# Where register loads stand, the order of VectorE's work in odd halves, and how many groups of rows come singly, in a graph-network kernel

## The chip, the core and the metric

The kernel runs on one core of a Trainium2 chip. The metric is the device time of one execution in microseconds. Before the change it is 3714.35 us, the median of 11 executions (3708.14 to 4204.9 us).

## What is computed

One layer of message passing on a graph of 12500 nodes with 128 features and 400000 edges sorted by destination, in float32. For node features x and edge features ea (32 wide):

```
h   = relu(layernorm(x))
m_e = relu(concat(h[src_e], h[dst_e], ea_e) @ w1 + b1) @ w2 + b2
agg = segment_sum(m, dst)
out = x + GRU(agg, h)          # gates from agg @ w_ih + b_ih and h @ w_hh + b_hh
```

The first product splits by rows of w1 into A[src] + B[dst] + ea @ w1e, with A = h @ w1a and B = h @ w1b.

## The kernel before, in words

**Set-up.** A first stage normalizes all nodes, keeps h transposed in SBUF (`hT_all`, 128 x 12500) and writes the table A (one row of 512 bytes for each node) to device memory.

**Tiling.** The 400000 edges are 3125 tiles of 128. Eight tiles make a double group k (391 of them): two groups a = 0, 1 of four tiles, whose destinations lie in two windows of 32 nodes that stand 8 nodes apart. A unit u is half a double group: u = 2k + h, four tiles, 512 edges. The main loop runs over the 782 units and issues, for each, pieces of several later units, so that the engines work in a pipeline. "Program unit u" below means what the loop issues in its round u. Instructions of an engine run in the order in which they were issued.

**One double group, step by step, with the rounds in which it is issued:**
- `fetch(q)` (lines 479 to 489) loads, on SP's queue and for two double groups at once, the edge features `L` (rows 64 to 127 of a 128-row tile, L485) and the destinations `Ld`, broadcast to 32 partitions in each of two DMAs (L488). Three buffers each. It is issued in round 4q - 8.
- `onehot_T(k)` (L495): VectorE compares Ld with node numbers; the result is the upper half of L. Round 2k - 6.
- `window(k)`: VectorE copies 64 columns of h (`hw`, L514) at a place from a register; TensorE multiplies them with w1b (L517). `window_rows(k)` (L526): VectorE adds b1 in two instructions, into `RW`, whose lower half holds w1e. Both are issued in even rounds, in phases 1 and 3 of the round.
- `onehot(k)` (L544): VectorE makes the one-hot matrix for the sum over destinations. Odd rounds, ahead of the add.
- `pre(u)` (L592): TensorE forms B[dst] + b1 + ea @ w1e of a unit in PSUM, from L and RW. Round u - 3.
- `add(u)` (L617): VectorE adds A's rows `G`. `relu(u)` (L623): ScalarE writes the activation. Round u - 2.
- `seg(u)` (L636): TensorE sums over destinations. `take(k)` (L644, L645) copies the sums out.
- Each 14 double groups, `node(b)` finishes 512 nodes (lines 648 to 727) in some 15 small steps, one in each round.

**How A's rows arrive.** There are four ways:
- POOL gathers them: eight indirect DMAs of 128 rows for a double group (L146), into a ring of 7 buffers.
- SP fetches them one row at a time: 1024 DMAs of 512 bytes (L795), each at an address from a register, into the only buffer `G_sp`.
- ScalarE (L788) or VectorE (L790) copies columns of h out of `hT_all`, one edge at a time, 128 x 4 bytes each, at a place from a register, 1024 for a double group. TensorE then multiplies these columns with w1a and adds them in PSUM (L603), and `add` is not needed.
- The first ten double groups gather rows of x and normalize them.

43 double groups come singly: 19 by ScalarE, 18 by VectorE, 6 by SP, spread by `SPREAD` from double group 30 on (lines 85 to 93). The registers are loaded 32 at a time (L782) from a table of indices in SBUF; the next 32 are loaded where the last of the 32 before have been used. A job (one double group's 1024 singles) starts in round 30 at the earliest and is spread evenly, in steps of 2 or 4 singles, over the four phases of its rounds (`run_jobs`). A job of SP for double group k ends by round 2k - 8, and the next may start in round 2k + 2, when the activation has read `G_sp`. SP's jobs cover the rounds 30 to 112, 122 to 232, 242 to 352, 362 to 472, 482 to 592 and 602 to 714.

**What sets the order.** No scheduler moves anything: the rounds, the four phases in a round and the calls in `stages` are the order. A round is: phase 0 of the jobs; `take`; `stages`; phase 1 (and `window`); phase 2; `seg`; phase 3 (and `window_rows`, and a step of `node`).

Of the kernel before, what the change touches and what calls it, by code (L numbers as in the profile page):

```python
# [8 lines left out]
F32 = mybir.dt.float32  # L9
# [33 lines left out]
PLACE = 20  # L43
CH = PLACE * PAIR
LOAD = 32
STEP = {"act": 4, "dve": 4, "sp": 2}
SPREAD = {"act": 19, "dve": 18, "sp": 6}
NR = 12672

H_AT = 16512  # L50
# [6 lines left out]
def tile_gnn(ctx: ExitStack, tc: tile.TileContext, x, src, srcT, dstT, dstP, eaT, eaP, w1, b1, w2T, b2,  # L57
# [26 lines left out]

    mode, order = {}, {m: [] for m in SPREAD}
    for m, n in SPREAD.items():
        lo = JOBS0 + 15
        for i in range(n):
            k = lo + int((i + 0.5) * (NP - 2 - lo) / n)
            while k in mode:  # L90
                k += 1
            mode[k] = m
            order[m].append(k)
# [385 lines left out]
    def fetch(q):  # L479
        if q * QP >= NP:  # L480
            return
        n = min(QP, NP - q * QP)
        Ls[q] = p3.tile([128, QP * 512], F32, name="L")
        c = slice(q * QP * 512, (q * QP + n) * 512)
        nc.sync.dma_start(Ls[q][2 * V:, :n * 512], eaP[:, c])  # L485
        Ds[q] = p3.tile([2 * V, QP * 512], I32, name="Ld")
        for a in range(2):
            nc.sync.dma_start(Ds[q][V * a:V * (a + 1), :n * 512],  # L488
                              dstP[a:a + 1, c].to_broadcast([V, n * 512]))
# [6 lines left out]
                                None, op0=ALU.is_equal)  # L496


    bases, PB_ = {}, {}

    def window(k):
        if k >= NP:
            return
        b = k // BP
        if k % BP == 0:
            n = min(BP, NP - k)
            _, vals = nc.values_load_multi_w_load_instructions(
                base_i[0:1, b, 0:n], engines=[ET.DVE], min_val=0, max_val=LAST,
                skip_runtime_bounds_check_because="clamped above")
            for i, v in enumerate(vals):  # L510
                bases[k + i] = v
        hw = p3.tile([128, 2, V], F32, name="hw", bufs=2)
        s = hT_all[:, bass.ds(bases.pop(k), V + SHIFT)]
        nc.vector.tensor_copy(hw, bass.AP(tensor=s.tensor, offset=s.offset,  # L514
                                          ap=[list(s.ap[0]), [SHIFT, 2], [1, V]]))
        PB_[k] = ps2.tile([128, 512], F32, name="oh")
        nc.tensor.matmul(PB_[k][:2 * V, :D], hw.rearrange("p a v -> p (a v)"), w1b,  # L517
                         start=True, stop=True)

    def window_rows(k):  # L520
        if k >= NP:
            return
        pm = PB_.pop(k)
        for a in range(2):
            s = slice(V * a, V * (a + 1))
            nc.vector.tensor_tensor(RW[k % 4][s, a, :], pm[s, :D], b1b[s, :], op=ALU.add)  # L526

    def onehot(k):
        if k >= NP:
            return  # L530
        t0, t1 = tiles(k)
        OH[k] = OHB[k % len(OHB)]
        for a in range(2) if k == 0 else (None,):
            if a is None:
                o, s = OH[k].rearrange("p j a v -> p a j v"), slice(t0, t1)
                d = dloc[:, s].rearrange("p (a j) -> p a j", a=2)[:, :, :, None]
                shape = [128, 2, GRP, V]
                i = iota[:, None, None, :]
            else:
                e = min(t1, (a + 1) * GRP)  # L540
                o, d = OH[k][:, :e - a * GRP, a, :], dloc[:, a * GRP:e, None]
                shape = [128, e - a * GRP, V]
                i = iota[:, None, :]
            nc.vector.tensor_tensor(o, d.to_broadcast(shape), i.to_broadcast(shape),  # L544
                                    op=ALU.is_equal)
# [222 lines left out]
        nc.sync.dma_start(at[r:r + 1, :], src[t0 * 128:(t0 + PAIR) * 128].rearrange(  # L768
            "(o e) -> o e", o=1))

    def one_by_one(m, k):
        et = {"act": ET.Activation, "dve": ET.DVE, "sp": ET.SP}[m]
        r = by_hand.index(k)
        if m == "sp":
            G[k] = pj[0].tile([128, GRP, 2, D], F32, name="G_sp", bufs=1)
            rows = G[k].bitcast(U8)
        else:
            hand[k] = pj[0].tile([128, PAIR * 128], F32, name=f"HE_{m}")
            he = hand[k].bitcast(U8)
        for e0 in range(0, PAIR * 128, LOAD):  # L780
            low, high = (0, ROW * (N - 1)) if m == "sp" else (H_AT, H_AT + 4 * (N - 1))
            _, vals = nc.values_load_multi_w_load_instructions(  # L782
                at[r:r + 1, e0:e0 + LOAD], engines=[et], min_val=low, max_val=high,
                skip_runtime_bounds_check_because="src holds numbers of nodes")
            for i, v in enumerate(vals):
                e = e0 + i
                if m == "act":
                    nc.scalar.copy(he[:, e * 4:e * 4 + 4], h_bytes[:, bass.ds(v - H_AT, 4)])  # L788
                elif m == "dve":
                    nc.vector.tensor_reduce(he[:, e * 4:e * 4 + 4],  # L790
                                            h_bytes[:, bass.ds(v - H_AT, 4), None],
                                            AX.X, ALU.max)
                else:
                    a, j = divmod(e // 128, GRP)
                    nc.sync.dma_start(rows[e % 128:e % 128 + 1, j, a, :],  # L795
                                      A_bytes[bass.ds(v, ROW)].rearrange("(o f) -> o f", o=1))
                if i % STEP[m] == STEP[m] - 1:
                    yield


    jobs = {}
    for m, kl in order.items():
        start = 2 * JOBS0
        for k in kl:
            end = 2 * k - (8 if m == "sp" else 4)
            jobs.setdefault(start, []).append((m, k, end - start))
            start = end if m != "sp" else 2 * k + 2
    live = {}

    PH = 4  # L810

    def run_jobs(u, phase):
        if u == 2 * JOBS0 and phase == 0:
            early.close()
            pj.append(late.enter_context(tc.tile_pool(name="pj", bufs=2, side="right")))
        if phase == 0:
            for m, k, span in jobs.get(u, ()):
                live[m] = [one_by_one(m, k), u, span, PAIR * 128 // STEP[m], 0]
        for m, job in list(live.items()):
            it, start, span, steps, done = job  # L820
            want = -(-steps * ((u - start) * PH + phase + 1) // (span * PH))
            while job[4] < want:
                job[4] += 1
                if next(it, "end") == "end":
                    del live[m]
                    break


    asked = [RAW]
# [9 lines left out]

    gathers(0)  # L840
    for q in range(2):
        fetch(q)
    for k in range(3):
        window(k)
        window_rows(k)


    def stages(u):
        if u + 7 >= 0:
            raw_stats(u + 7)  # L850
        if u + 6 >= 0:
            raw_fin(u + 6)
            raw_h(u + 6)
        if u % 2 == 0:
            onehot_T(u // 2 + 3)
        elif u > -7:
            onehot(u // 2 + 3)
        if u + 4 >= 0:
            raw_turn(u + 4)
        if u + 3 >= 0:  # L860
            pre(u + 3)
        if u + 2 >= 0:
            add(u + 2)
            relu(u + 2)

    for u in range(-7, 0):
        stages(u)
# [12 lines left out]
    for u in range(NU):  # L880
        k, h = divmod(u, 2)
        gathers(u)
        if h == 0:
            if k % QP == 0:
                fetch(k // QP + 2)
            if k % BP == 0 and k:
                nodes_left.append([node(k // BP - 1), 0])
            if k % PLACE == 1:
                indices(k // PLACE + 2)
            if k % PLACE == 5:  # L890
                place(k // PLACE + 1)
                dst_tile(k // PLACE + 2)
            if k == NP - 20:
                check_windows()
        for r in range(2 * u, min(2 * u + 2, NJ)):
            job_indices(r)
        if u == 2 * JOBS0 - 2:
            nc.vector.tensor_scalar(at, at, place_of[:, 0:1], place_of[:, 1:2],
                                    op0=ALU.mult, op1=ALU.add)

        def other(phase):
            run_jobs(u, phase)
            if h == 0 and phase == 1:
                window(k + 3)
            if h == 0 and phase == 3:
                window_rows(k + 3)
            if phase == 3:
                step(nodes_left)

        other(0)  # L910
        if h == 0:
            take(k - 1)
        stages(u)
        other(1)
        other(2)
        seg(u)
        if u == 0:
            node_setup()
        other(3)
# [173 lines left out]
```

## Time and profile before

| | |
|---|---|
| median of 11 | 3714.35 us |
| the profiled execution | 3722.88 us, of which its span is 3721.1 us |
| mean TensorE clock granted | 0.78 |
| POOL's gathers from A | 2704, 0.956 us each, 0.30 us apart |
| ScalarE's single copies | 19456, 189 ns each, overlapping; 1966.1 us busy in all |
| VectorE's single copies | 18432, 146 ns each, overlapping; 1338.4 us busy in all |
| VectorE's adds of A's rows | 676, 683 ns each |
| SP's single rows | 6144, from 224.5 to 3430.6 us |
| idle time of POOL that ended with ScalarE's activation | 181.8 us |

The span is one execution on the chip. "Busy" counts the time in which an engine had at least one operation running; overlapping ones count once. "Issue" as the end of an idle time means that nothing the profile shows ended it: the engine's sequencer was occupied. Register loads and the issuing of DMAs run on the sequencers and are not counted as busy. "SPq" is SP's sequencer.

### The profile page before, as it was taken

The page shows a single profiled execution, that of the slowest core. Times are in us where ns is not written, and L with a number is a line of the kernel's source. Part 1 is how long each engine was busy: PE and PEld are TensorE (multiplying, and loading weights), DVE is VectorE, ACT ScalarE, POOL GpSimd, SP SyncE. Part 2 cuts the span into 40 slices and gives each one's busy share as a digit, 9 for nine tenths or more (in the row PEclk, how much of TensorE's full clock was granted, in tenths as well). Part 3 has the DMA queues.
Part 4 walks back from the last instruction along what each step waited for, and adds up shares of the span by engine and source line. Part 5 has one row for each costly group of instructions (what it writes and reads, how often), then busy time and mean ns, then how long its engine had stood idle before and what let it go on. Part 6 is the DMA issues. An engine that isn't in the chain of part 4 may idle for free. (4 is left out here: it accounts for less than half of the span.)

```text
span 3721.1 us, 94893 instructions
## 1 busy us (share of the span) xinstructions
PE 2652.2 (71%) x13578; PEld 1641.5 (44%) x13578; DVE 2629.5 (71%) x22515; ACT 2515.5 (68%) x20936; POOL 2657.9 (71%) x2789
## 2 busy tenths in 40 slices
PE   6684665767776777677777767777776677677768
PEld 6452333444443444444444434444444444344435
DVE  7765556677777676767777777777777777777774
ACT  5455556667677777767777776777777777767772
POOL 7677646477777677777777777677777677777775
PEclk9897777777777877877787777777877877787779
DMA  6333222233333333333333333333333333333332
GB/s 201 83 92 81 74 66 75 71 90 84 90 85 89 81 87 86 87 86 87 94 86 87 87 90 84 81 88 88 93 88 89 81 89 86 89 84 90 86 87 65
DMA packets 157887, 325.92 MB, mean 88 GB/s; under 512 B 65058, under 2 KB 77133, under 8 KB 157256
## 3 DMA queue, kind: packets, MB, share of 16 engines
q0 software_dynamic: 88992, 182.43, 19.5%
q1 hardware_dynamic: 68119, 137.33, 13.8%
q14 instruction: 520, 4.25, 0.4%
q8 instruction: 112, 1.84, 0.2%
q10 hardware_dynamic: 144, 0.07, 0.0%
HBM read 305.74 MB, written 13.84 MB: 86 GB/s over the span
## 5 line engine op out<-in xcount | busy, mean ns | idle before, releaser
L146 POOL DMA_INDIRECT G<-A,src_i x2704 | 2583.9, 956 | 1005.7 <-issue 769.0
L788 ACT COPY HE_act<-hT_all 128x4 uint8 x19456 | 1966.1, 189 | 584.7 <-issue 582.0
L790 DVE TENSOR_REDUCE HE_dve<-hT_all 128x4 uint8 x18432 | 1338.4, 146 | 718.5 <-issue 708.3
L592 PE MATMUL pre<-RW,L 128*128 128x256 f32 x3128 | 1141.8, 494 | 131.1 <-DVE G L617 99.6
L592 PEld LDWEIGHTS pre<-RW,L 128*128 128x128 f32 x3128 | 681.8, 242 | 439.2 <-issue 295.4
L517 PE MATMUL oh<-w1b,hw 128*64 128x128 f32 x782 | 210.8, 360 | 893.1 <-DVE hw L514 889.0
L623 ACT ACTIVATE RB<-G 128x512 f32<-128x512 f32 x676 | 424.8, 628 | 335.3 <-DVE G L617 84.5
L636 PE MATMUL seg<-RB,OH 128*32 128x129 f32 x6250 | 646.5, 342 | 0.0
L517 PEld LDWEIGHTS oh<-w1b,hw 128*64 128x64 f32 x782 | 90.2, 163 | 1046.2 <-DVE hw L514 1023.8
L617 DVE TENSOR_TENSOR G<-pre,G 128x512 f32<-128x512 f32 x676 | 461.7, 683 | 10.1 <-PE pre L592 0.3
L636 PEld LDWEIGHTS seg<-RB,OH 128*32 128x32 f32 x6250 | 351.0, 131 | 236.7 <-issue 137.5
L495 DVE TENSOR_SCALAR L<-Ld,node_of 64x512 f32<-64x512 int32 x391 | 192.0, 491 | 86.2 <-DMA Ld<-in_dstP 70.9
L526 DVE TENSOR_TENSOR RW<-oh,b1b 32x128 f32<-32x128 f32 x782 | 217.4, 278 | 48.4 <-PE oh L517 39.9
L644 DVE COPY sums<-seg 64x128 f32<-64x128 f32 x391 | 107.6, 275 | 84.0 <-PE seg L636 78.8
L544 DVE TENSOR_TENSOR OH<-dloc,iota 128x256 f32<-128x256 f16 (+1 forms) x392 | 162.6, 415 | 0.5 <-issue 0.2
L667 PEld LDWEIGHTS nd<-spot,sums 64*128 64x128 f32 x782 | 152.7, 300 | 12.9 <-issue 12.9
L667 PE MATMUL nd<-spot,sums 64*128 64x40 f32 x782 | 156.8, 385 | 0.0
L645 ACT CAST dcol<-seg 64x1 f16<-64x1 f32 x391 | 59.3, 152 | 136.8 <-DVE sums L644 136.3
L631 PE MATMUL seg<-zrow 1*64 1x129 bf16 x391 | 106.4, 272 | 0.0
L146 POOL DMA_INDIRECT G<-in_x,src_i x77 | 73.0, 948 | 25.1 <-issue 22.9
L514 DVE COPY hw<-hT_all 128x64 f32 x391 | 82.5, 211 | 11.1 <-issue 8.3
L631 PEld LDWEIGHTS <-zrow 1*64 1x64 bf16 x391 | 43.4, 111 | 93.2 <-issue 93.2
(151 smaller groups left out, 1521.4 us busy)
## 6 DMA issues: line engine op xcount, KB each, us to landing
G_sp<-A SPq DMA_DIRECT2D x6144, 0.5 KB
L<-in_eaP SPq DMA_DIRECT2D x195, 256.0 KB
Ld<-in_dstP SPq DMA_DIRECT2D x390, 128.0 KB
G<-A,src_i POOLq DMA_INDIRECT x2704
xb<-in_x SPq DMA_DIRECT2D x28, 256.0 KB
out<-xb SPq DMA_DIRECT2D x28, 256.0 KB
xs<-in_x SPq DMA_DIRECT2D x11, 512.0 KB
A<-asb SPq DMA_DIRECT2D x11, 512.0 KB
```

What stands on the lines that cost most here:

```text
L146: nc.gpsimd.indirect_dma_start(out=G[k][:, j, a, :], out_offset=None, in_=table, in_offset=bass.IndirectOffsetOnAxis(ap=src_i[c][:, i:i + ...
L495: nc.vector.tensor_scalar(Ls[k // QP][:2 * V, c], Ds[k // QP][:, c], node_of[:, k:k + 1], None, op0=ALU.is_equal)
L517: nc.tensor.matmul(PB_[k][:2 * V, :D], hw.rearrange("p a v -> p (a v)"), w1b, start=True, stop=True)
L526: nc.vector.tensor_tensor(RW[k % 4][s, a, :], pm[s, :D], b1b[s, :], op=ALU.add)
L544: nc.vector.tensor_tensor(o, d.to_broadcast(shape), i.to_broadcast(shape), op=ALU.is_equal)
L592: nc.tensor.matmul(PP[u][:, 2 * i:2 * i + 2, :], Ls[k // QP][:, c0:c0 + 128], RW[k % 4], start=True, stop=not raw)
L617: nc.vector.tensor_tensor(RT[u], PP.pop(u), RT[u], op=ALU.add)
L623: nc.scalar.activation(o[:, :, :D], RT.pop(u), AF.Relu)
L636: nc.tensor.matmul(SEG[k][V * a:V * (a + 1), :D + 1], OH[k][:, j, a, :], RB[u % 3][:, (j % 2) * 2 + a, :D + 1], start=False, stop=all(b != ...
L667: nc.tensor.matmul(pt[:, bass.ds(offs[i], V + SHIFT)], sums[:, i, :], spot, start=False, stop=i == n - 1)
L788: nc.scalar.copy(he[:, e * 4:e * 4 + 4], h_bytes[:, bass.ds(v - H_AT, 4)])
L790: nc.vector.tensor_reduce(he[:, e * 4:e * 4 + 4], h_bytes[:, bass.ds(v - H_AT, 4), None], AX.X, ALU.max)
```

## The change

- 49 double groups come singly: 22 by VectorE, 20 by ScalarE, 7 by SP. Their places are spread anew. VectorE's jobs start in round 31, ScalarE's in 47, SP's in 30. SP's jobs now cover the rounds 30 to 134, 144 to 238, 248 to 340, 350 to 444, 454 to 548, 558 to 650 and 660 to 754.
- VectorE's and ScalarE's jobs load 32 registers once in a round: VectorE's load stands after the add (and, in odd rounds, after the bias adds and the one-hot) and the last 7 singles of the 32 before; ScalarE's after the activation and the last 8. The other singles are spread over the four phases. SP loads as before and issues its rows evenly.
- `window`'s copy moves into even rounds ahead of the add, its matmul (`window_b`) stays in phase 1, and the bias adds (`window_rows`) move into the odd round after the add. `onehot` moves after the add too.
- The loads of Ld (`fetch_d`) are split from those of L and issued one fetch, four rounds, earlier; within a round they stand ahead of L's.

```diff
-STEP = {"act": 4, "dve": 4, "sp": 2}
-SPREAD = {"act": 19, "dve": 18, "sp": 6}
+
+TAIL = {"dve": 7, "act": 8}
+SPREAD = {"dve": 22, "act": 20, "sp": 7}
...
-        lo = JOBS0 + 15
+        lo, hi = {"dve": (JOBS0 + 3, NP - 14), "act": (JOBS0 + 11, NP - 6),
+                  "sp": (JOBS0 + 5, NP - 10)}[m]
         for i in range(n):
-            k = lo + int((i + 0.5) * (NP - 2 - lo) / n)
+            k = lo + int((i + 1) * (hi - lo) / n)
...
+        c = slice(q * QP * 512, (q * QP + n) * 512)
         Ls[q] = p3.tile([128, QP * 512], F32, name="L")
+        nc.sync.dma_start(Ls[q][2 * V:, :n * 512], eaP[:, c])
+
+    def fetch_d(q):
...
-        nc.sync.dma_start(Ls[q][2 * V:, :n * 512], eaP[:, c])
         Ds[q] = p3.tile([2 * V, QP * 512], I32, name="Ld")
...
+        HW[k] = hw
+
+    def window_b(k):
+        if k >= NP:
+            return
         PB_[k] = ps2.tile([128, 512], F32, name="oh")
-        nc.tensor.matmul(PB_[k][:2 * V, :D], hw.rearrange("p a v -> p (a v)"), w1b,
+        nc.tensor.matmul(PB_[k][:2 * V, :D], HW.pop(k).rearrange("p a v -> p (a v)"), w1b,
                          start=True, stop=True)
...
+    def behind(m, u):
+        if m in live:
+            live[m].run()
+            if live[m].e == PAIR * 128:
+                del live[m]
+        begin(m, u + 1)
+        if m in live:
+            j = live[m]
+            if j.loaded < PAIR * 128:
+                j.load(LOAD)
...
+    PARTS = (1, 2, 3, 0)
 
     def run_jobs(u, phase):
...
+        for m in ("act", "dve"):
+            if m in live:
+                n = max(0, len(live[m].vals) - TAIL[m])
+                live[m].run(TAIL[m] + n - -(-n // (4 - PARTS.index(phase))))
         if phase == 0:
...
+            begin("sp", u)
+        if "sp" in live:
+            j = live["sp"]
+            want = -(-PAIR * 128 * ((u - j.start) * 4 + phase + 1) // (j.span * 4))
+            while j.e < want:
+                if not j.vals:
+                    j.load(LOAD)
+                j.run(max(0, len(j.vals) - (want - j.e)))
...
         if u % 2 == 0:
             onehot_T(u // 2 + 3)
-        elif u > -7:
-            onehot(u // 2 + 3)
+            if u >= 0:
+                window(u // 2 + 3)
...
         if u + 2 >= 0:
             add(u + 2)
+        if u % 2 and u > -7:
+            if u > 0:
+                window_rows(u // 2 + 3)
+            onehot(u // 2 + 3)
+        if u + 2 >= 0:
+            behind("dve", u)
             relu(u + 2)
+            behind("act", u)
...
             if k % QP == 0:
+                fetch_d(k // QP + 3)
                 fetch(k // QP + 2)
...
         def other(phase):
             run_jobs(u, phase)
             if h == 0 and phase == 1:
-                window(k + 3)
-            if h == 0 and phase == 3:
-                window_rows(k + 3)
+                window_b(k + 3)
```

More of the change, by code (lines that the diff above doesn't have):

```diff
@@ L482, in fetch @@
         n = min(QP, NP - q * QP)
+        c = slice(q * QP * 512, (q * QP + n) * 512)
         Ls[q] = p3.tile([128, QP * 512], F32, name="L")
+        nc.sync.dma_start(Ls[q][2 * V:, :n * 512], eaP[:, c])
+    def fetch_d(q):
+        if q * QP >= NP:
+            return
+        n = min(QP, NP - q * QP)
         c = slice(q * QP * 512, (q * QP + n) * 512)
-        nc.sync.dma_start(Ls[q][2 * V:, :n * 512], eaP[:, c])
         Ds[q] = p3.tile([2 * V, QP * 512], I32, name="Ld")
@@ L496, in onehot_T @@
                                 None, op0=ALU.is_equal)
-    bases, PB_ = {}, {}
+    bases, PB_, HW = {}, {}, {}
     def window(k):
@@ L515, in window @@
                                           ap=[list(s.ap[0]), [SHIFT, 2], [1, V]]))
+        HW[k] = hw
+    def window_b(k):
+        if k >= NP:
+            return
         PB_[k] = ps2.tile([128, 512], F32, name="oh")
-        nc.tensor.matmul(PB_[k][:2 * V, :D], hw.rearrange("p a v -> p (a v)"), w1b,
+        nc.tensor.matmul(PB_[k][:2 * V, :D], HW.pop(k).rearrange("p a v -> p (a v)"), w1b,
                          start=True, stop=True)
@@ L769, in job_indices, with __init__, load, run @@
             "(o e) -> o e", o=1))
[L771 to L780, printed above, removed]
+    class Job:
+        def __init__(self, m, k, start, span):
+            self.m, self.k, self.start, self.span = m, k, start, span
+            self.e, self.loaded, self.vals = 0, 0, []
+            self.r = by_hand.index(k)
+            if m == "sp":
+                G[k] = pj[0].tile([128, GRP, 2, D], F32, name="G_sp", bufs=1)
+                self.to = G[k].bitcast(U8)
+            else:
+                hand[k] = pj[0].tile([128, PAIR * 128], F32, name=f"HE_{m}")
+                self.to = hand[k].bitcast(U8)
+        def load(self, n):
+            m = self.m
             low, high = (0, ROW * (N - 1)) if m == "sp" else (H_AT, H_AT + 4 * (N - 1))
+            et = {"act": ET.Activation, "dve": ET.DVE, "sp": ET.SP}[m]
             _, vals = nc.values_load_multi_w_load_instructions(
-                at[r:r + 1, e0:e0 + LOAD], engines=[et], min_val=low, max_val=high,
+                at[self.r:self.r + 1, self.loaded:self.loaded + n], engines=[et],
+                min_val=low, max_val=high,
                 skip_runtime_bounds_check_because="src holds numbers of nodes")
-            for i, v in enumerate(vals):
-                e = e0 + i
+            self.vals = list(vals)
+            self.loaded += n
+        def run(self, left=0):
+            while len(self.vals) > left:
+                v, e, m, to = self.vals.pop(0), self.e, self.m, self.to
+                self.e += 1
                 if m == "act":
-                    nc.scalar.copy(he[:, e * 4:e * 4 + 4], h_bytes[:, bass.ds(v - H_AT, 4)])
+                    nc.scalar.copy(to[:, e * 4:e * 4 + 4], h_bytes[:, bass.ds(v - H_AT, 4)])
                 elif m == "dve":
-                    nc.vector.tensor_reduce(he[:, e * 4:e * 4 + 4],
+                    nc.vector.tensor_reduce(to[:, e * 4:e * 4 + 4],
                                             h_bytes[:, bass.ds(v - H_AT, 4), None],
@@ L794, in one_by_one, with begin @@
                     a, j = divmod(e // 128, GRP)
-                    nc.sync.dma_start(rows[e % 128:e % 128 + 1, j, a, :],
+                    nc.sync.dma_start(to[e % 128:e % 128 + 1, j, a, :],
                                       A_bytes[bass.ds(v, ROW)].rearrange("(o f) -> o f", o=1))
-                if i % STEP[m] == STEP[m] - 1:
-                    yield
-    jobs = {}
+    starts = {}
     for m, kl in order.items():
-        start = 2 * JOBS0
+        start = 2 * JOBS0 + (m != "sp") + (16 if m == "act" else 0)
         for k in kl:
             end = 2 * k - (8 if m == "sp" else 4)
-            jobs.setdefault(start, []).append((m, k, end - start))
+            starts[m, start] = (k, end - start)
             start = end if m != "sp" else 2 * k + 2
     live = {}
-    PH = 4
+    def begin(m, u):
+        if (m, u) in starts:
+            live[m] = Job(m, starts[m, u][0], u, starts[m, u][1])
+    def behind(m, u):
[8 more added lines that the diff above has]
+                j.load(LOAD)
+            assert j.span * LOAD >= PAIR * 128
+    PARTS = (1, 2, 3, 0)
     def run_jobs(u, phase):
@@ L815, in run_jobs @@
             pj.append(late.enter_context(tc.tile_pool(name="pj", bufs=2, side="right")))
+        for m in ("act", "dve"):
+            if m in live:
+                n = max(0, len(live[m].vals) - TAIL[m])
+                live[m].run(TAIL[m] + n - -(-n // (4 - PARTS.index(phase))))
         if phase == 0:
[L817 to L826, printed above, removed]
+            begin("sp", u)
[6 more added lines that the diff above has]
+                j.run(max(0, len(j.vals) - (want - j.e)))
+            if j.e == PAIR * 128:
+                del live["sp"]
     asked = [RAW]
@@ L841, in tile_gnn @@
     for q in range(2):
+        fetch_d(q)
         fetch(q)
+    fetch_d(2)
     for k in range(3):
         window(k)
+        window_b(k)
         window_rows(k)
```

## The prediction

> **What bounds the kernel now.** I read the page's first table, the waits by engine in two windows, the timeline of SP's queue, and last the sizes of the register loads.
>
> The busy table alone names no bound: four engines stand at 68 to 71%.
>
> ```profile
> PE 2652.2 (71%) x13578; PEld 1641.5 (44%) x13578; DVE 2629.5 (71%) x22515; ACT 2515.5 (68%) x20936; POOL 2657.9 (71%) x2789
> ...
> L788 ACT COPY HE_act<-hT_all 128x4 uint8 x19456 | 1966.1, 189 | 584.7 <-issue 582.0
> L790 DVE TENSOR_REDUCE HE_dve<-hT_all 128x4 uint8 x18432 | 1338.4, 146 | 718.5 <-issue 708.3
> ```
>
> The two hand lines carry 582 and 708 us of idle time that nothing released ("issue"). The view of the load line says what it is: a register load that holds the engine's sequencer.
>
> ```profile
> L782 ACTq TENSOR_LOAD <-at x608: 1965/1990/2512, 226.1 to 3617.3; - x152
> L782 DVEq TENSOR_LOAD <-at x576: 2097/2118/2729, 230.4 to 3622.6; - x192
> L782 SPq TENSOR_LOAD <-at x192: 1872/2127/2318, 222.2 to 3415.1; - x192
> ```
>
> So 708.3/576 = 1.23 us of each 2.12 us load is bare on VectorE and 582/608 = 0.96 us of 1.99 on ScalarE; the rest lies under operations that were already queued (up to 10 of them start after the load does).
>
> SP is not in the busy table, since issuing is not counted. Its timeline in the first job (units 30 to 112, 224.5 to 693.5 us) is full:
>
> ```profile
> 467.25 20.15 SPq L795 DMA_DIRECT2D G_sp<-A  x50
> 487.51 0.48 SPq L485 DMA_DIRECT2D L<-in_eaP  x1
> 488.04 1.04 SPq L488 DMA_DIRECT2D Ld<-in_dstP  x2
> 491.29 8.45 SPq L795 DMA_DIRECT2D G_sp<-A  x26
> ```
>
> 1024 rows, 32 loads and 20 fetches took 469.0 us, and the waits of SP in 230 to 690 us name hardly anything but its own DMAs. In 250 to 690 us VectorE waits for SP's one-hot indices, 15 times; these are all such waits of the run:
>
> ```profile
> DVE L L495 <- DMA Ld<-in_dstP: 70.9, 15, 7.6
> ```
>
> In that stretch POOL is busy 0.65 and VectorE 0.58 of the time, and a unit takes 5.7 us. **There SP sets the time.** In the five later jobs it nearly does: 500.9, 502.7, 497.4, 492.5 and 504.2 us for 110 units (the last 112), of which SP waited 2 to 11 us for another engine. Less these, 491 to 493 us. There the computing engines set the time, at some 4.55 us a unit. Between jobs SP is free for 34.8, 51.4, 45.3, 53.7 and 54.4 us, since the next job's first row waits for the activation that reads the last G_sp.
>
> **The change, part by part.**
>
> *Loads and VectorE's extra jobs.* VectorE gets 4 jobs more: 4096 reduces x 72.6 ns (1338.4/18432) = +297 us. ScalarE gets one: 1024 x 101 ns (1966.1/19456) = +103 us. The loads become 704 and 640. VectorE's now stands behind the add (683 ns) and 7 reduces at a 64 ns pitch with a tail of 0.08, so 1.2 us are covered where the add waits for PE, and up to 1.9 us where one-hots, window copy or bias adds are queued too. Of 2.12 us plus 0.09 of restart, 0.3 to 1.0 stay bare; I take 0.6 (of the rows of before, those with an add and reduces queued, 0.44 and 0.58 us bare, are nearest): 704 x 0.6 = 422 us against 708. ScalarE's stands behind the activation (628 ns) and 8 copies at 95 ns; before shows such loads 0.49 to 0.55 us bare, so 320 us against 582. VectorE nets about +10 us and ScalarE -160. If the cover is gone the loads keep 1.23 us, +160 us more on VectorE.
>
> Per unit, VectorE had 1.44 us of other work, 1.87 of reduces, 0.98 bare load and 0.25 of waits = 4.55. Afterwards it has 31.4 reduces a unit: 1.44 + 2.28 + 0.6 + 0.25 = 4.57 us.
>
> *POOL.* 48 gathers fewer, each 0.95 + 0.30 us: -60 us. From double group 15 to 377 it needs 314 x 8 x 1.25/724 = 4.34 us a unit, so POOL is no longer last.
>
> *Odd halves, window and bias.* The same instructions in another order. The add comes 0.97 us earlier (two 278 ns bias adds and a 415 ns one-hot), the matmul of B waits less for its window copy (889 us idle on PE before, but only 40 us passes on, as VectorE's wait for it). I bound this by 0 and -0.25 us a unit, VectorE's whole waits. It is worth nothing where SP sets the time.
>
> *fetch_d.* Same DMAs; the index rows are asked for four units earlier. VectorE needs them at program unit 4q-6 of fetch q, issued at 4q-8 before and 4q-12 now. So where SP lags, the others can run not 2 but 5 units ahead of it, the limit then being the edge attributes (issued 4q-8, needed by PE at 4q-3). SP's own stall after each fetch stays: it reuses eight completion marks in turn, so the eighth DMA after a fetch waits for its landing (about 5.4 us after the first issue). The same 512 KB are in flight either way.
>
> *The seventh SP job.* This decides. 1024 rows, 32 loads more; and each job gets fewer units. From 469.0 us at 82 units and 492 at 110, a job of n units costs SP 469.0 + 0.82 (n - 82). The new jobs have 104, 94, 92, 94, 94, 92 and 94 units: 487 + 4 x 478.8 + 2 x 477.2 = 3357 us. That is 5.1 us a unit in six of seven jobs, over all three engines' needs (4.57 at most). Nothing hides it: SP has no other cover, and the others queue behind its fetches.
>
> Between jobs SP waits until ScalarE has read G_sp, at program unit 2k-1, having ended at 2k-8. Computing that leads by 5 units has 2 left, 2 x 4.6 us plus 4 for landing and pipeline: 13. Before, computing trailed by 3: (7+3) x 4.5 = 45 plus some 6, which matches 51. I allow 20 for the first and 14 for the others, as node phases fall into some: 90 us, with bounds of 54 (9 each) and 210 (the shortest of before, 35 each).
>
> Sum: 224.5 (first row, pinned by the release of the early buffers) + 3357 + 90 = 3671 us at program unit 754, with the others at about 759. In before that point, the activation of unit 761, comes at 3642 us, 79 before the end; nothing late in the kernel is dearer now and POOL is no longer behind, so 75. Span 3746, and 1.8 around it: 3748 us. The profiled execution took 3722.88 us, 8.5 over the median of 3714.35; the ratio 1.0067 gives 3739, say **3738 us**.
>
> [...] Here 50 rows took SP 20.15 us to issue, 0.40 each, with no other engine in the way. [...]
>
> **Rivals.**
>
> *Faster: SP's stalls shrink.* Rows waiting for the landing of L or Ld cost SP 81.9 + 46.1 us in 730 to 3430 us and 19 in the first job: 147 us, 24.5 a job, 172 us in seven. With Ld issued first, L last, the waits could overlap better. All gone: about 3566 us; half gone: 3652. From 31 us saved on, the change is faster. Against it: the last of the three transfers gates either way.
>
> *Slower still: VectorE sets the time.* If the load's cover fails because the sequencer sits in the add's wait, bare time is 1.0 to 1.23 us and a unit 4.97 to 5.2. From 4.72 a unit on, the cycle of 104 units (491) is no longer SP's 493, and at 4.95 the run is 224.5 + 724 x 4.95 + 75 = 3883. Between, 3770 to 3830. Speaking for it: 31.4 reduces a unit leave VectorE no spare.
>
> *No change.* The first job's gain (units 30 to 134 in 487 us, where before takes some 557) and the later loss (5.1 for 4.55 us a unit, less shorter pauses) cancel: 3707 to 3722 us. This takes pauses of 9 to 10 us.
>
> **How the numbers follow.** A measurement of this kernel can tell about 0.2% from no change, 7.4 us. SP as summed: 0.6, 3715 to 3765 us, of which 0.06 lies within 0.2%. Faster: 0.18. VectorE: 0.12. No change: 0.10, of which 0.01 just under. So faster 0.19, same 0.15, slower 0.66. The range leaves out the lower half of the faster case and the upper part of VectorE's: 3655 to 3795.
>
> **What would show it.** If right: SP's timeline has rows without a gap in all seven jobs, each 475 to 490 us long, pauses of 10 to 20 us; SP's waits for PE at the fetch are near zero; VectorE's wait for Ld is gone and PE waits for the edge attributes L instead; POOL's idle behind ScalarE's activation is well over 181.8 us; issue idle on the hand lines is some 420 us (VectorE) and 320 (ScalarE), with the busy shares of both still under 80%. Wrong would be: jobs well under 470 us (stalls shrank), or SP waiting for PE within jobs while VectorE is never idle (computing sets it).

## The result, and the profile after

The changed kernel takes **3820.9 us** (median of 8 executions, 3819.0 to 3826.99). The kernel before took 3713.66 us, the median of 31 executions (the first 11 of them are those of the table above). The ratio is 1.0291, with a 95% interval of 1.0276 to 1.0306: **slower by 2.9%**, 83 us above the forecast and 26 us above the upper end of its range. The profiled execution's span is 3816.2 us.

From the page of the changed kernel, the busy table and the two hand lines (busy us and mean ns, then the idle time before them and what ended most of it):

```profile
PE 2737.0 (72%) x13658; PEld 1697.7 (44%) x13658; DVE 2887.8 (76%) x26601; ACT 2620.1 (69%) x21960; POOL 2611.6 (68%) x2741
...
L814 ACT COPY HE_act<-hT_all 128x4 uint8 x20480 | 2069.6, 189 | 467.6 <-issue 450.4
L816 DVE TENSOR_REDUCE HE_dve<-hT_all 128x4 uint8 x22528 | 1579.5, 146 | 708.1 <-issue 704.7
```

A load is called covered for the time in which operations that stood ahead of it still run on its engine, and bare for the time in which the engine then has nothing to run. VectorE is busy 258 us longer than before, and its idle time behind loads has not fallen: 704.7 us against 708.3. A load was bare 1.23 us and is bare 704.7/704 = 1.00 us, but there are 128 more of them. ScalarE's went from 584.7/608 = 0.96 to 467.6/640 = 0.73 us. A VectorE load itself takes what it took (median 2129 ns, 2118 before).

From the waits of the changed kernel (total us, times, longest): POOL now stands behind ScalarE, and ScalarE behind VectorE.

```profile
POOL G L148 <- ACT RB L636: 321.7, 75, 19.8
ACT dcol L658 <- DVE sums L657: 280.2, 121, 7.5
ACT RB L636 <- DVE G L630: 201.2, 150, 3.5
```

POOL waited 181.8 us for the activation before, and ScalarE waited less for VectorE's copy of the sums and for its add. The two lines of before:

```profile
ACT dcol L645 <- DVE sums L644: 136.3, 69, 7.9
ACT RB L623 <- DVE G L617: 84.5, 64, 7.8
```

From 1000 to 3500 us VectorE is busy 1922.76 us and stands 503.7 us behind loads: 97% of the time, where the same two make 94% of 1000 to 3400 us before. A unit takes 4.81 us there (units 122 to 752 in 3033 us): 3.70 us busy, 0.97 behind loads, 0.14 waiting.

One even and one odd half in VectorE's timeline of the changed kernel (start us, us, and in brackets the idle time ahead):

```profile
2401.84 0.27 DVE L657 COPY sums<-seg 64x128 f32<-64x128 f32 x1
2402.04 0.50 DVE L503 TENSOR_SCALAR L<-Ld,node_of 64x512 f32<-64x512 int32 x1
2402.47 0.17 DVE L522 COPY hw<-hT_all 128x64 f32 x1
2402.56 0.67 DVE L630 TENSOR_TENSOR G<-pre,G 128x512 f32<-128x512 f32 x1
2403.16 0.52 DVE L816 TENSOR_REDUCE HE_dve<-hT_all 128x4 uint8 x7
2404.11 1.68 DVE L816 TENSOR_REDUCE HE_dve<-hT_all 128x4 uint8 x25 [0.42 <-issue]
2405.71 0.68 DVE L630 TENSOR_TENSOR G<-pre,G 128x512 f32<-128x512 f32 x1
2406.30 0.56 DVE L539 TENSOR_TENSOR RW<-oh,b1b 32x128 f32<-32x128 f32 x2
2406.88 0.42 DVE L557 TENSOR_TENSOR OH<-dloc,iota 128x256 f32<-128x256 f16 x1
2407.22 0.53 DVE L816 TENSOR_REDUCE HE_dve<-hT_all 128x4 uint8 x7
2409.11 0.22 DVE L816 TENSOR_REDUCE HE_dve<-hT_all 128x4 uint8 x2 [1.36 <-issue]
```

In the even half the load is issued 0.02 us after the copy L657 starts. Ten operations wait behind that copy, 1.80 us are covered and 0.41 stay bare (medians of 243 loads). In the odd half the load is not issued when the add L630 starts, but 0.02 us after the one-hot L557 does: 0.86 us are covered by the one-hot and the seven singles, and **1.36 us stay bare** (medians of 345 loads, 477 us in all). The add and the bias adds, 1.24 us of cover, are over by then.

### The profile page after: what moved, and what is told of

The parts are those of the page before. It is cut to its first block, busy times and chain, and to the rows that moved or that the text cites. A ratio compares the mean times of both kernels' runs of the same rounds, so it can differ in the third digit from the quotient of the medians.

```text
span 3816.2 us, 102399 instructions
## 1 busy us (share of the span) xinstructions
PE 2737.0 (72%) x13658; PEld 1697.7 (44%) x13658; DVE 2887.8 (76%) x26601; ACT 2620.1 (69%) x21960; POOL 2611.6 (68%) x2741
## 5 line engine op out<-in xcount | busy, mean ns | idle before, releaser
L148 POOL DMA_INDIRECT G<-A,src_i x2656 | 2537.6, 955 | 1128.7 <-issue 749.6
L814 ACT COPY HE_act<-hT_all 128x4 uint8 x20480 | 2069.6, 189 | 467.6 <-issue 450.4
L816 DVE TENSOR_REDUCE HE_dve<-hT_all 128x4 uint8 x22528 | 1579.5, 146 | 708.1 <-issue 704.7
L605 PE MATMUL pre<-RW,L 128*128 128x256 f32 x3128 | 1205.8, 516 | 88.4 <-ACT RB L636 56.0
L605 PEld LDWEIGHTS pre<-RW,L 128*128 128x128 f32 x3128 | 711.1, 253 | 411.9 <-issue 218.9
L649 PE MATMUL seg<-RB,OH 128*32 128x129 f32 x6250 | 671.1, 352 | 1.0 <-ACT RB L636 1.0
L636 ACT ACTIVATE RB<-G 128x512 f32<-128x512 f32 x664 | 417.0, 628 | 317.6 <-DVE G L630 201.2
L649 PEld LDWEIGHTS seg<-RB,OH 128*32 128x32 f32 x6250 | 362.0, 135 | 258.2 <-issue 181.5
L630 DVE TENSOR_TENSOR G<-pre,G 128x512 f32<-128x512 f32 x664 | 449.5, 679 | 7.2 <-PE pre L605 6.6
L657 DVE COPY sums<-seg 64x128 f32<-64x128 f32 x391 | 110.0, 281 | 90.6 <-PE seg L649 81.7
L557 DVE TENSOR_TENSOR OH<-dloc,iota 128x256 f32<-128x256 f16 (+1 forms) x392 | 167.1, 427 | 5.4
L644 PEld LDWEIGHTS <-zrow 1*64 1x64 bf16 x391 | 43.7, 112 | 96.5 <-issue 96.5
```

The lines of the kernel that those rows point to most:

```text
L148: nc.gpsimd.indirect_dma_start(out=G[k][:, j, a, :], out_offset=None, in_=table, in_offset=bass.IndirectOffsetOnAxis(ap=src_i[c][:, i:i + ...
L605: nc.tensor.matmul(PP[u][:, 2 * i:2 * i + 2, :], Ls[k // QP][:, c0:c0 + 128], RW[k % 4], start=True, stop=not raw)
L630: nc.vector.tensor_tensor(RT[u], PP.pop(u), RT[u], op=ALU.add)
L636: nc.scalar.activation(o[:, :, :D], RT.pop(u), AF.Relu)
L649: nc.tensor.matmul(SEG[k][V * a:V * (a + 1), :D + 1], OH[k][:, j, a, :], RB[u % 3][:, (j % 2) * 2 + a, :D + 1], start=False, stop=all(b != ...
L814: nc.scalar.copy(to[:, e * 4:e * 4 + 4], h_bytes[:, bass.ds(v - H_AT, 4)])
```

## The experiments

Two theories. **VectorE**: the bare loads of the odd halves make VectorE the last engine at 4.81 us a unit. **SP**: as predicted, SP's seventh job sets the time. Ratios are to the kernel before, run beside each experiment (medians 3711.64 to 3713.05 us), with 95% intervals. "Issue idle" is VectorE's idle time behind loads.

**e1, one SP job less.**

```diff
-SPREAD = {"dve": 22, "act": 20, "sp": 7}
+SPREAD = {"dve": 22, "act": 20, "sp": 6}
```

> SP has 6 jobs instead of 7, of about 110 rounds each; POOL gathers the seventh's double group; everything else is as in the changed kernel (3820.9 us). Theory SP (the prediction: the time SP takes to issue the single rows sets the pace): each round needs SP 4.45 us instead of 5.1, so the run falls by 100 us or more, to 3720 or below. Theory VectorE (VectorE's own stream of singles and bare register loads sets the pace at 4.8 us a round): no change, 3805 to 3830, with SP waiting for buffers at its fetches within the jobs.

Measured: 3825.6 us, ratio 1.0294 (1.0264 to 1.0324), as the changed kernel. A seventh of SP's rows is gone and nothing is gained. SP's waits in the changed kernel, and then in e1:

```profile
SPq L496 <- DVE hw L522: 168.8, 31, 18.6
```

```profile
SPq L496 <- DVE hw L522: 533.5, 139, 19.7
```

SP has 1024 rows less to issue and waits 365 us longer at the fetch, until VectorE has used what the next transfer overwrites. SP does not set the time of the changed kernel.

**e2, the last seven singles ahead of the bias adds, the load behind the one-hot.** The same instructions; the tail and the load are split:

```diff
             add(u + 2)
+        if u + 2 >= 0:
+            behind("dve", u)
         if u % 2 and u > -7:
             if u > 0:
                 window_rows(u // 2 + 3)
             onehot(u // 2 + 3)
         if u + 2 >= 0:
-            behind("dve", u)
+            load_next("dve", u)
```

> In odd rounds the last 7 singles stand directly behind the add, then the bias adds and the one-hot, and the register load last; even rounds, counts and SP's jobs are unchanged. In the changed kernel's trace 345 of 352 loads in odd rounds are issued only when the one-hot starts, with 7 singles (0.45 us) queued, and 1.36 us of each stay bare; here add, bias adds and one-hot (1.6 us) should lie over the load. Theory VectorE: about 1.1 us less in each of 352 odd rounds, 390 us off VectorE's stream, until SP's jobs (3340 us and pauses) set the time: 3720 to 3750 us. Theory SP: VectorE has slack, no change, 3810 to 3830.

Measured: 3724.4 us, ratio 1.0028 (1.0014 to 1.0041), 96 us below the changed kernel. The page's hand line and an odd half of e2:

```profile
L816 DVE TENSOR_REDUCE HE_dve<-hT_all 128x4 uint8 x22528 | 1574.7, 146 | 379.2 <-issue 375.3
```

```profile
2404.70 0.68 DVE L630 TENSOR_TENSOR G<-pre,G 128x512 f32<-128x512 f32 x1
2405.30 0.53 DVE L816 TENSOR_REDUCE HE_dve<-hT_all 128x4 uint8 x7
2405.74 0.56 DVE L539 TENSOR_TENSOR RW<-oh,b1b 32x128 f32<-32x128 f32 x2
2406.32 0.42 DVE L557 TENSOR_TENSOR OH<-dloc,iota 128x256 f32<-128x256 f16 x1
2406.94 1.68 DVE L816 TENSOR_REDUCE HE_dve<-hT_all 128x4 uint8 x25 [0.20 <-issue]
```

Now the load goes out 0.05 us after the add starts, with ten operations waiting: covered 2.00 us, bare 0.24 (medians of 303 loads). VectorE saves 329 us, the run only 96. What took over is what the prediction described, and its terms can be read off SP's rows:

| us | predicted | changed kernel | e2 |
|---|---|---|---|
| first row of SP | 224.5 | 219.4 | 219.6 |
| seven jobs | 3357 | 3339.6 | 3327.6 |
| six pauses between them | 90 | 160.3 | 94.8 |
| from the last row to the end | 75 | 96.9 | 87.4 |
| span | 3746 | 3816.2 | 3729.4 |

The wait that the prediction named as its sign stands in e2 and is all but absent (1.8 us, 2 times) in the changed kernel:

```profile
PE pre L605 <- DMA L<-in_eaP: 361.7, 78, 9.7
```

**e3, both edits (e1's and e2's).**

> Both edits. If both streams lie close under one another, each alone is held by the other and only both together release the time: theory VectorE with SP next: 3500 to 3600 us (POOL at 4.4 us a round next). Theory SP alone: the same as with 6 jobs alone. Theory VectorE without SP: the same as with the tail first alone.

Measured: **3520.4 us**, ratio 0.9464 (0.9433 to 0.9495): 5.4% faster than the kernel before, and the best of all kernels here. With VectorE's loads covered, SP's seventh job costs 3724.4 - 3520.4 = 204 us; with them bare it costs nothing (e1).

**e4, the new order with the old counts and places** (19, 18 and 6):

> The changed order of loads, windows, bias adds, one-hots and fetches, but 19, 18 and 6 jobs at the double groups of before. Since a job now uses 32 registers a round, it is done in 32 of its 38 to 40 rounds. It parts the change's order from its counts. Theory VectorE: bare load 0.4 us in even and 1.36 in odd rounds, 0.9 on average against 1.23 before, 576 x 0.33 = 190 us off VectorE's stream: faster than before's 3714, 3560 to 3680 us; the 18 to 22 jobs of VectorE are then what costs. Theory SP: SP's jobs are those of before, so 3690 to 3720 us.

Measured: 3732.6 us, ratio 1.0046 (1.0031 to 1.0062). The 3560 to 3680 us that the VectorE theory gave were missed, and the 3690 to 3720 us of the SP theory by 13 us: a load is bare 585.8/576 = 1.02 us, about as in the changed kernel, and the run is no faster than the kernel before. VectorE's two largest waits in e4:

```profile
DVE HE_dve L815 <- issue: 585.8, 592, 1.9
DVE sums L656 <- PE seg L648: 286.2, 111, 16.9
```

The first job of SP still ends at 681.7 us (before at 693.5): there SP is the limit, and VectorE waits. After it, a job of VectorE now lasts 32 rounds, one load in each, and there is one in 38 to 40 rounds. In e4's trace a unit takes 4.70 us while a job of VectorE runs and 4.47 us between two jobs (counted by the activations, from the fourth job on), so the rounds between do not make up for it. Why they are no faster, though VectorE is idle in 2.1 of those 4.47 us, was not tested.

**e5, e4 with e2's edit.**

> The changed kernel with two edits: the last seven singles of an odd half run ahead of the bias adds and one-hot and the load stands behind the one-hot (as in e2), and the counts and places of the kernel before (19, 18, 6 singly gathered double groups). Theory (VectorE's bare load is what the changed order costs; with it gone the engines named next set the time): bare loads fall from e4's 586 us to some 190 (576 x 0.33), VectorE needs about 1.44 + 1.85 + 0.26 + 0.25 = 3.8 us a unit and is no longer last; POOL needs some 4.42 us a unit and SP's first job stays as long as in e4 (ends near 681 us). So 681 + 622 units x 4.42 + some 97 = 3530 us if POOL alone sets the rest, up to 3640 us with the activation and VectorE alternating: 3530 to 3640. Rival (the old counts leave VectorE enough room, and the order of the tail is worth nothing there): within 0.5% of e4, 3715 to 3750, with SP's first job and the places setting the time.

Measured: 3618.4 us, ratio 0.9744 (0.9727 to 0.9761), in the theory's range, 114 us below e4; a load is bare 0.53 us. So the odd half's load costs that much with the old counts too.

**e6, the one-hot back ahead of the add; e7, four singles instead of seven behind the one-hot in odd halves.** Both ask what holds the load back. The edits:

```diff
-        if u + 2 >= 0:
-            add(u + 2)
         if u % 2 and u > -7:
-            if u > 0:
-                window_rows(u // 2 + 3)
             onehot(u // 2 + 3)
+        if u + 2 >= 0:
+            add(u + 2)
+        if u % 2 and u > 0:
+            window_rows(u // 2 + 3)
```

```diff
-                n = max(0, len(live[m].vals) - TAIL[m])
-                live[m].run(TAIL[m] + n - -(-n // (4 - PARTS.index(phase))))
+                left = 4 if m == "dve" and (u + (phase > 0)) % 2 else TAIL[m]
+                n = max(0, len(live[m].vals) - left)
+                live[m].run(left + n - -(-n // (4 - PARTS.index(phase))))
```

> The changed kernel with the one-hot of an odd half back ahead of the add (add, bias adds, seven singles, load follow). Theory A (the load's issue is held until the operation just ahead of the singles starts, whatever it is): load issued at the second bias add's start, cover 0.28 + 0.55 = 0.8 us, bare 1.4 as in the changed kernel; no change, 3800 to 3840 us. Theory B (it is the one-hot, which waits for data of its own, that holds the queue): the load is issued at the add's start with nine operations waiting, cover 1.8 us or more, bare 0.3 to 0.5 in odd rounds; issue idle on the hand line falls from 705 to some 350 to 400 us and SP sets the time as in e2: 3715 to 3750 us.

> The changed kernel, but in odd halves four instead of seven singles are left to stand between the one-hot and the load. Theory A (the load's issue is held until the one-hot starts): the cover shrinks to 0.42 + 4 x 0.064 + 0.08 = 0.75 us, bare 1.45 instead of 1.36 in odd rounds, some +30 us of issue idle: 3830 to 3870 us. Theory C (a limit in places: too many singles behind the one-hot hold it back): the load is issued at the add's or a bias add's start, bare 0.3 to 0.8 us, issue idle down by 150 to 350 us, 3720 to 3790 us.

Measured: e6 3927.5 us (1.0578, 1.0561 to 1.0596), e7 3885.2 us (1.0463, 1.0445 to 1.0482). Neither the one-hot by itself nor the number of singles holds the load. In e7 it still goes out as the one-hot starts, with four singles waiting instead of seven; bare 1.55 us. In e6 it goes out even later, as the second bias add ends and the first single starts, so that only 0.52 us are covered:

```profile
2403.18 0.56 DVE L539 TENSOR_TENSOR RW<-oh,b1b 32x128 f32<-32x128 f32 x2
2403.76 0.54 DVE L816 TENSOR_REDUCE HE_dve<-hT_all 128x4 uint8 x7
2405.98 1.68 DVE L816 TENSOR_REDUCE HE_dve<-hT_all 128x4 uint8 x25 [1.69 <-issue]
```

Theory A of e6 missed the time (3800 to 3840) and the moment (the start of the second bias add), theory B the sign. In all three kernels (the changed one, e6 and e7) the load comes 0.60 us after the first bias add starts. Theory A of e7 had the moment right; the time lies 15 us above its range.

**e8, the kernel before with the new counts and places alone.**

> The kernel before with the change's counts and places alone (22, 20 and 7 singly gathered double groups), its order of operations and its register loads where they were. Theory (VectorE sets the time of the changed kernel, and the new order does lower its bare load from 1.23 to 1.00 us): 704 x 1.23 = 866 us bare instead of 705, VectorE 1.44 + 2.28 + 1.20 + 0.25 = 5.17 us a unit, some 161 to 260 us above the changed kernel: 3950 to 4080 us. Rival (the order is worth nothing, the counts make all of the loss): 3800 to 3840 us as in the changed kernel. Rival (SP's seventh job sets the time, as the prediction had it): 3720 to 3765 us.

Measured: 4047.7 us, ratio 1.0905 (1.0885 to 1.0925), as the VectorE theory said. The hand line of e8:

```profile
L791 DVE TENSOR_REDUCE HE_dve<-hT_all 128x4 uint8 x22528 | 1596.6, 145 | 946.2 <-issue 939.7
```

So the change is two opposite things: the counts alone cost 335 us, and at these counts the new order gives 227 us back. At the old counts it gives nothing (e4).

**e9 and e10, where the bias adds stand** (both with six SP jobs). e9: add, one-hot, singles, load, bias adds. e10: bias adds, one-hot, add, singles, load.

```diff
         if u % 2 and u > -7:
-            if u > 0:
-                window_rows(u // 2 + 3)
             onehot(u // 2 + 3)
         if u + 2 >= 0:
             behind("dve", u)
+        if u % 2 and u > 0:
+            window_rows(u // 2 + 3)
+        if u + 2 >= 0:
             relu(u + 2)
```

```diff
-        if u + 2 >= 0:
-            add(u + 2)
         if u % 2 and u > -7:
             if u > 0:
                 window_rows(u // 2 + 3)
             onehot(u // 2 + 3)
         if u + 2 >= 0:
+            add(u + 2)
             behind("dve", u)
```

> The changed kernel with six SP jobs instead of seven (so that VectorE's time shows), and in odd halves the bias adds behind the load: add, one-hot, seven singles, load, bias adds. Known beside it: bias adds and one-hot ahead of the singles and load 3826 us (bare 1.36 us a load in odd halves), both between singles and load 3520 us (bare 0.24). Theory D (singles that follow the bias adds are held until the second bias add is done): with no bias add ahead, the load is issued at the add's start with eight operations waiting, cover 0.68 + 0.42 + 0.53 = 1.6 us, bare 0.5: some 3570 to 3620 us. Theory E (they are held behind any such operation of another kind, the one-hot too): the load is issued when the first single starts, cover 0.53, bare 1.7, and the time is 3860 to 3930 us as with the one-hot back ahead of the add; where the one-hot's start releases it, cover 0.9, bare 1.3: 3790 to 3830 us.

> The changed kernel with six SP jobs, and in odd halves the add last of the long operations: bias adds, one-hot, add, seven singles, load. Theory D (held until the second bias add is done, the one-hot's start): cover 0.42 + 0.68 + 0.53 = 1.6 us, bare 0.5: 3570 to 3620 us. Theory F (only the number of waiting operations, ten, counts): the load is issued when the first bias add starts, cover 2.1, bare 0.1 to 0.2: 3480 to 3530 us. Theory E (held until the operation just ahead of the singles starts, here the add): cover 0.68 + 0.53 = 1.2, bare 0.9 to 1.0: 3680 to 3740 us.

Measured: e9 3618.8 us (0.9743, 0.9726 to 0.9759), e10 3764.3 us (1.0137, 1.0120 to 1.0154). In e9 nothing holds the load: in 231 of the 352 odd halves it goes out just ahead of the add, with ten operations waiting, and is bare 0.67 us. But the bias adds now come too late and wait themselves; VectorE's waits in e9:

```profile
DVE HE_dve L816 <- issue: 218.8, 360, 1.8
DVE RW L539 <- issue: 121.0, 144, 1.6
DVE sums L657 <- PE seg L649: 88.4, 54, 12.3
DVE RW L539 <- PE seg L649: 73.4, 99, 1.3
DVE RW L539 <- PE pre L605: 65.7, 85, 1.2
```

The issue idle is that of e3, 218.8 + 121.0 = 340 us, and 73.4 + 65.7 = 139 us of new waits for PE stand beside it; the run takes 98 us longer than e3. Theory D had e9's time (3570 to 3620) right, but not the moment (the add's start). In e10 the load goes out 0.02 us after the add starts, not when the one-hot does (336 loads, 1.11 us bare in the median): theory D (0.5) and theory F (0.1 to 0.2) are out. Theory E has the place right for e10, with the time 24 us above its range, but it is wrong for e9 and e6. None of the three holds for all.

**The sum over all pairs.** Where VectorE sets the time, the time follows its issue idle. The lines of e1, e3, e6, e7 and e10, in this order (the others are shown above):

```profile
DVE HE_dve L816 <- issue: 709.5, 719, 1.8
DVE HE_dve L816 <- issue: 351.3, 714, 1.8
DVE HE_dve L816 <- issue: 824.5, 718, 2.4
DVE HE_dve L816 <- issue: 772.2, 719, 2.2
DVE HE_dve L816 <- issue: 638.4, 719, 1.8
```

| pair | issue idle, us | time, us |
|---|---|---|
| e8 - changed | +235.0 | +226.8 |
| e6 - changed | +119.8 | +106.6 |
| e7 - changed | +67.5 | +64.3 |
| e10 - e1 | -71.1 | -61.3 |
| e3 - e1 | -358.2 | -305.2 |
| e9 - e1 | -369.7, and +139.1 of waits for PE | -206.9 |
| e2 - changed | -329.4 | -96.5 (then SP sets it) |

Six pairs give 0.85 to 0.97 us of time (e9's net, 0.90) for each us of bare load. That is the VectorE theory, up to the point where SP becomes the last engine (e2).

## Why the prediction was wrong

**The step that failed** is the price of VectorE's load: "Of 2.12 us plus 0.09 of restart, 0.3 to 1.0 stay bare; I take 0.6". Measured: 1.00 in the mean, the very end of that interval, made of 0.63 in even halves and 1.37 in odd ones (means over 352 loads each). The even half was judged well. The odd half was expected to have the better cover, "up to 1.9 us where one-hots, window copy or bias adds are queued too", and has 0.86. The rows I called nearest (0.44 and 0.58) were the wrong ones: they have the copy of the sums ahead of the add. The trace of before also held 61 loads that stood behind a one-hot, an add and four singles, and those went out only when the add had started, 1.28 us bare. They were the nearest rows to a load behind one-hots, and would have warned. One of them (the load goes out at 2156.46 us):

```profile
2156.00 0.41 DVE L544 TENSOR_TENSOR OH<-dloc,iota 128x256 f32<-128x256 f16 x1
2156.44 0.69 DVE L617 TENSOR_TENSOR G<-pre,G 128x512 f32<-128x512 f32 x1
2157.05 0.34 DVE L790 TENSOR_REDUCE HE_dve<-hT_all 128x4 uint8 x4
2158.65 0.47 DVE L790 TENSOR_REDUCE HE_dve<-hT_all 128x4 uint8 x6 [1.26 <-issue]
```

The "+160 us more on VectorE" for a cover that is gone counts from the loads of before; from the 422 us of the sum it would be 704 x 1.23 - 422 = 444 us.

**Hence "1.44 + 2.28 + 0.6 + 0.25 = 4.57 us"** came out as 3.70 + 0.97 + 0.14 = 4.81: the work was right, the load 0.37 too small, the waits 0.11 too large.

**"This decides" (the seventh SP job)** does not hold in the changed kernel (e1: nothing gained without it), and does in e2 and e3 (204 us). That the change is slower was forecast rightly, but by luck: the forecast had it from this job. The job lengths were right: six of 471.0 to 476.7 us and the first of 496.5, for 477 to 487 predicted. The pauses were not: 54.1 us and then 16.2 to 24.7, 160 in all for 90, and the tail was 97 for 75. These two terms carry the whole miss of the span: 92 us too small, while the jobs and the first row were 22 us too large, which leaves the 70 us between 3746 and 3816.2. Both rest on "Computing that leads by 5 units". Here computing trails by 3 at the end of the first job (SP waits 16 us for VectorE in that job and 44 us in the pause behind it), leads by 3 to 5 at the end of the next five and by 1 at the end of the last. In e2, where the same count gives a lead of 5 to 6 in all seven, the sum of 3746 stands against 3729.4.

**The price of a row.** In the changed kernel the seventh job is free (e1), but not because its rows cost nothing: in e3 against e2 the same 1024 rows cost 204 us, 0.20 us each. The prediction's count of SP's time by rows (50 in 20.15 us, 1024 and what goes with them in 469.0 us) priced SP rightly (seven jobs of 3327.6 us in e2 for 3357); what was wrong was which engine is last.

**The rivals.** *Slower still: VectorE sets the time* is what happened, and 3820.9 us lies in its interval "3770 to 3830", at a chance of 0.12. Its threshold was right: "From 4.72 a unit on" against SP's 490 us for 104 units in e2, 4.71. Its mechanism was not: the sequencer does not sit in the add's wait. VectorE waits only 6.6 us for PE at the add in the whole run. *Faster* and *No change* are out; SP's stalls for L and Ld did shrink, to 109.1 + 19.5 us from 147, but its jobs of 471 us and more are not "well under 470".

**The other steps.** ScalarE: bare 0.73 for "0.49 to 0.55"; 296 loads have 0.54, but 257 go out 0.2 us after the activation's start and have 0.92 (ScalarE now waits 201.2 us for VectorE's add there; that this is the reason was not tested). It is not the last engine. POOL is no longer last: right, 321.7 us of waiting. *fetch_d*: VectorE's wait for Ld is gone; that PE waits for L instead is right in e2 (361.7 us) and not in the changed kernel (1.8 us). SP's stall after a fetch stayed, though shorter: in the changed kernel's trace SP's DMAs use eight semaphores in turn, and in 112 of the 165 fetches between 230 and 3430 us SP stands idle, 0.96 us in the median, ahead of the eighth DMA after that of L. The odd halves' order was bounded by 0 and 0.25 us a unit of waits; its real effect was on the load's cover, which I did not price: putting the one-hot alone back ahead costs 107 us (e6).

**Still open** is why the load is held in odd halves. With the bias adds ahead of the singles and the load, it goes out when the second bias add is done (changed kernel, e6, e7), or, in e10, when the one-hot behind them is done; four, six or seven operations wait at that moment. The 61 loads of before, behind bias adds, singles, one-hot, add and four singles, go out when the one-hot is done, as in e10. With the singles ahead of the bias adds (e2), or the bias adds behind the load (e9), it goes out with ten waiting. The product that the bias adds read was ready about 3 us before they started (median; changed kernel and e6), so it is no wait for data that the trace shows. No fixed number of waiting operations fits either: in the even halves ten start after the load does, in e7's odd halves four.

## What to carry to other kernels

In this kernel a register load cost what its cover left bare, and the cover runs from the moment at which the load is issued (covered and bare add up to 1.80 + 0.41 = 2.21 us in even halves and to 0.86 + 1.36 = 2.22 us in odd ones). That moment can come later than the place of the load in the program suggests (in odd halves after the 1.24 us of add and bias adds). So read from the timeline, for each place of a load, which operations start after it, and price each place by itself and not by a mean. Then try the order: here the same instructions with the singles directly behind the add and the load last (e2's edit) were worth 96 us, and 305 us with one SP job less. When work is dealt out among engines, add the bare loads to each engine's busy time before the paces are compared: at the new counts and in the old order the six groups moved cost 335 us, more than the 227 us that the new order brought back.

## What the runs showed of the hardware

- Ten operations that stood ahead of a load had not started on VectorE when the load was issued (even halves; e2; e9); in all twelve kernels there were more in 25 of 8064 loads, eleven each time.
- The same operations in another order decide when a load is issued: bare 0.24 us in e2 and 1.36 us in the changed kernel (medians of 303 and 345 loads), with the load behind the same eleven instructions.
- A load of 32 registers takes VectorE 2.12 to 2.13 us and ScalarE 1.99 to 2.01 us (medians of the kernel before, the changed one and e8): the order changes what of it is bare, not the load.
